# The joining products of the second image every fourth scan step and no longer every second

## The chip, the cores and the metric

The kernel runs on one core of a Trainium2 chip. The metric is the device time of one execution in microseconds, from launch to end; it includes little beside the span between the first and the last instruction. The engines are TensorE (PE), VectorE (DVE), ScalarE (ACT), GpSimd (POOL), and SyncE (SP), whose queue issues most of the DMA transfers. Each engine works through its own queue in program order, and waits at an instruction until what it depends on has been signalled.

## The reference, cut to what matters

The input x is (4, 256, 32, 32) in fp32: 4 images of 256 channels and 1024 tokens. One layer is a convolutional block with a residual, and then a layer of experts with a residual:

```python
x = x + conv_block(ln_over_channels(x))
t = tokens(x)                         # 4 x 1024 rows of 256
t = t + experts(layernorm(t))         # top 2 of 8, 256 -> 1024 -> 256, GELU

# conv_block, for each image
xn = layernorm(x)
xm = four mamba scans over 64 channels each (16 states) + skip * xn
... gates and convolutions along the tokens give xm2
x_local  = conv1d(xm2)                # over the tokens, per channel
x_global = attention(xm2)             # 8 heads, 1024 tokens
x_out = concat(x_local, x_global) @ fc_w.T + fc_b     # the joining product, 512 -> 256
x_out = gelu(layernorm(x_out))
xi = ln_over_the_image(x_out), then a 3x3 convolution per channel
x_mixed = layernorm(xi) @ proj_w.T + proj_b
```

## The kernel before, in words

**Layout.** Channels lie on the 128 partitions in two blocks (`c` or `co`), tokens along the free axis in two halves of 512 (`h`). One PSUM bank holds one 128x512 fp32 tile; the eight banks are handed out by `ps(name)` from one pool, each in turn as its last reader lets it go. Buffers of one half in SBUF come from `a2`, of 1024 tokens from `a4`, of both blocks from `a8`.

**The scan sets the tick.** The mamba scans of an image are 8 parts, four channel groups by two halves of the tokens, of 16 steps each (one state each). A step of a part is: ACT makes dA (L732), PE makes bs, the input factors (L724), DVE multiplies dBu (L742) and runs the recurrence (L753), POOL multiplies the result by the output factors (L761), and PE sums over the states (yp, L766 and L771). Round the parts come the smaller jobs of each channel group: up products and silu (L630 to L660, with its table load), softplus of dt on ACT (L675 to L678) and its sums on POOL (L682, L686).

**All else is laid between the steps.** The whole program is written in a manually ordered schedule: instructions are in each engine's queue in the order in which Python issues them. Every other job is a generator. After each scan step `beat()` raises the tick by one and lets each running generator go on until it yields; `yield n` means "not again for n steps". So a job's yields decide behind which scan step its instructions stand in each queue. Behind the fourth scan part of an image (from the second image on) the attention of the image before is started, then `joined`, in one chain. So the second image is joined in the third image's fifth part. Outside the scans (in the attention stage, and at the end) beats go on without steps.

**The joined product.** `joined(b)` makes four products (`CO_H`: two output blocks by two halves) with `in_turn`. Each product is four matmuls 128x128 by 128x512 (L428), into one PSUM bank; ACT copies it with a bias into `xc` (L1286). `in_turn` makes one item per turn, uses the one made `lag // every` turns ago, and yields `every` steps per turn. For the second image (b = 1) the lag is 4.

**What hangs on it.** After the last turn `joined` sets the flag `("joining", b)`. Then it takes the deviation over the channels (`inverse_deviation`: squares on ACT, mean on PE, `root` on ACT at L419 and L420, multiplies on DVE at L1269) and the Gelu (L1295, with a table load, and another back, L413). The flag also releases `sent_off(b - 1)`, that is `sent_off(0)` for image 1 when the second image is joined (`behind_flag`): it loads the residual xr (1 MB, L1361), takes off the mean and the deviation (L1355, L1269), makes the four proj products (`pr`, L426 and L428), whose copies add the bias on ACT (L1373). Then comes the dispatch to the experts: transposes of the rows (`raw`, L1836), their copies to XR on ACT (L1828), statistics on DVE (L1843, L1844), the store of Y, the gate product (L1867), the routing, and sixteen scatters of XR's rows to HBM on POOL's queue, one every two steps, each with a memset (L1974, L1975). POOL has these beside its scan multiplies of the end of the third image and the start of the fourth; there too lie the third image's convolutions, with taps on DVE (L462).

Of the kernel before, what the change touches and what calls it, by code (L numbers as in the profile page):

```python
# [78 lines left out]
def network(  # L79
# [46 lines left out]
    def col(name, i=0, rows=slice(0, P)):  # L126
        at = _AT[name] + i
        return V[rows, at : at + 1]
# [22 lines left out]
    with tc.tile_pool(name="w_conv", bufs=1) as wp, tc.tile_pool(  # L151
# [239 lines left out]
        def a8(name, shape=(P, NC2, N)):  # L391
            return act8.tile(list(shape), F32, tag="a8", name=name)
# [13 lines left out]
        def half(h):  # L406
            return ts(h, HALF)
# [3 lines left out]
        def log_exp():  # L411
            if loaded[0] != LOG_EXP:
                nc.scalar.preload_act_table_set(LOG_EXP)  # L413
                loaded[0] = LOG_EXP
# [7 lines left out]
        def product(name, w, co, chunks, kept=None, at=0):  # L422

            out = ps(name)
            if kept is not None:
                nc.tensor.matmul(out, ident, kept, start=True, stop=False)  # L426
            for ci, chunk in enumerate(chunks):
                nc.tensor.matmul(  # L428
                    out, w[:, at + ci, ts(co, P)], chunk, start=(ci == 0 and kept is None),
                    stop=(ci == len(chunks) - 1),  # L430
                )
            return out
# [10 lines left out]
        def in_turn(items, make, use, lag=2, every=1):  # L443

            made, lag = [], lag // every
            for at in range(len(items) + lag):
                if at >= lag:
                    use(items[at - lag], made[at - lag])
                if at < len(items):
                    made.append(make(items[at]))  # L450
                yield every
# [772 lines left out]
        def pace(b, ticks):  # L1224

            if b == B - 1:
                T["pace",] = ticks

        def inverse_deviation(name, xc, alone, quick=False):

            r = a4(f"r_{name}")

            def squares(h):
                sq = [a2(f"sq_{name}_{h}_{c}") for c in range(NC2)]
                for c in range(NC2):
                    nc.scalar.activation(sq[c], xc[:, c, half(h)], AF.Square)
                return sq

            if alone:
                sq = [squares(h) for h in range(2)]  # L1240
                var = []
                for h in range(2):
                    yield 1
                    var.append(column_mean(f"var_{name}_{h}", sq[h]))
                yield 1
                for h in range(2):
                    root(r[:, half(h)], var[h], eps5)
                yield 1
            elif quick:
                sq, var = [], []  # L1250
                for at in range(6):
                    if at < 2:
                        sq.append(squares(at))
                    if 2 <= at < 4:
                        var.append(column_mean(f"var_{name}_{at - 2}", sq[at - 2]))
                    if 4 <= at:
                        root(r[:, half(at - 4)], var[at - 4], eps5)
                    yield 1
            else:
                for h in range(2):  # L1260
                    sq = squares(h)
                    yield 1
                    var = column_mean(f"var_{name}_{h}", sq)
                    yield 2
                    root(r[:, half(h)], var, eps5)
                    yield 1
                yield 1
            for c in range(NC2):
                nc.vector.tensor_tensor(xc[:, c, :], xc[:, c, :], r, ALU.mult)  # L1269
                yield 1  # L1270

        def joined(b):

            xloc, oT = XLOC.pop(b), OT.pop(b)
            pace(b, PACE["product"])
            T["attending", b] = True
            while b == B - 2 and not T.get(("projected", b - 1)):
                yield 1
            xc = XC[b] = a8(f"xc_{b}")
            both = [xloc[:, ci, :] for ci in range(NC2)] + oT  # L1280
            yield from in_turn(
                CO_H, lambda at: product(
                    f"fc_{b}_{at[0]}_{at[1]}", fcT_s, at[0],
                    [v[:, half(at[1])] for v in both],
                ),
                lambda at, r: nc.scalar.activation(  # L1286
                    xc[:, at[0], half(at[1])], r, AF.Identity, bias=fcb[:, at[0] : at[0] + 1]
                ), lag=(4, 4, 2, 2)[b], every=(4, 2, 2, 1)[b],
            )

            T["joining", b] = True
            pace(b, PACE["norm"])
            yield from inverse_deviation(f"lgn_{b}", xc, b == B - 1)
            for c in range(NC2):
                nc.scalar.activation(  # L1295
                    xc[:, c, :], xc[:, c, :], AF.Gelu, bias=col("lgn_b", c), scale=col("lgn_w", c)
                )
            loaded[0] = None
            if b < B - 1:
                log_exp()  # L1300
            yield 2
# [280 lines left out]
        with tc.manual_schedule(engines=ALL):  # L1582
# [4 lines left out]
            for b in range(B):  # L1587
                for p in range(PARTS):
# [15 lines left out]
                    if b > 0 and p == PARTS // 2 - 1:  # L1604
                        drain()
                        start(
                            one_by_one(attention(b - 1), joined(b - 1)), finish_part(at),
                            one_by_one(
                                local(b - 1), *([around(b - 2)] if b > 1 else []),
                                *([normalised(b + 1)] if 1 < b < B - 1 else []),  # L1610
                            ),
                        )
                        if b == B - 1 and b in XD:
                            start(taps_ahead(b))
                        if b > 1:
                            flag = "attending" if b == B - 1 else "joining"
                            start(behind_flag((flag, b - 1), sent_off(b - 2)))
                        if b == 1:
                            start(normalised(b + 1))
                        while not T.get(("attended", b - 1)):  # L1620
                            beat()
                        resume(at + 1)
# [12 lines left out]
            until("attended", B - 1, 2)  # L1635
            T["hold",] = False
            start(one_by_one(joined(B - 1), around(B - 1), sent_off(B - 1)))
            if not shifted:
                start(judged())
# [912 lines left out]
```

## Time and profile before

| | us |
|---|---|
| median of 3 runs | 2160.07 |
| lowest, highest | 2158.35, 2161.26 |
| profiled execution, its own time | 2160.25 |
| its span, first to last instruction | 2158.5 |
| PE, DVE, ACT, POOL busy | 1921.5, 1539.0, 1212.5, 1052.9 |
| mean granted PE clock | 0.963 |

The profile is of one execution. A line of its timeline is: start, duration, engine, source line, operation, output and inputs, shape, count of instructions drawn together; in brackets, the idle time of the engine just before, and what ended it. In a line of windows, the columns are the stretch, its length, the busy time (and count) of PE, PE's weight loads, DVE, ACT and POOL, then the granted PE clock, the busy share of the DMA engines, and GB/s. The line with one digit per slice gives the busy share in tenths for 40 equal slices of the span. Instructions of one kind that follow each other are drawn as one line, and the ends of matmuls are modelled.

The four products stand at 906, 915, 920 and 927 us in the third image's fifth part; the transposes of the first image's dispatch begin at 987, its scatters lie between 1033 and 1108, and the fourth image's first scan step is at 1045.

### The profile page before, as it was taken

What the parts mean: (1) busy time and instruction counts of PE and PEld (TensorE: products, weight loads), DVE (VectorE), ACT (ScalarE), POOL (GpSimd) and SP (SyncE); (2) the same over time, 40 slices, a digit from 0 to 9 for tenths busy, and PEclk for the clock granted to TensorE, in tenths of its full rate; (3) what the DMA queues carried; (4) which work ended last, traced back from release to release, by engine and by line L of the source; (5) the groups of instructions that cost most, each with busy time, mean ns of one, the idle gap of its engine ahead of it and who ended that gap; (6) DMA issues with size and microseconds to landing.
All of it is one profiled execution on the core that took longest, in us unless ns stands there. A gap on an engine that the chain in (4) does not pass through costs nothing. (4 is left out here: it accounts for less than half of the span.)

```text
span 2158.5 us, 28179 instructions
## 1 busy us (share of the span) xinstructions
PE 1921.5 (89%) x8682; PEld 866.5 (40%) x8682; DVE 1539.0 (71%) x2253; ACT 1212.5 (56%) x2274; POOL 1052.9 (49%) x935
## 2 busy tenths in 40 slices
PE   6778778999887999988789999769999989999996
PEld 2112112322211232223123223226743768888885
DVE  3999999876999989789889898986265345221121
ACT  4665657678676667677466876625267423222221
POOL 0787887731887850376878016752031012422131
PEclk8888999999999999998999999999999999999998
DMA  3665544311454431053734203445230166877764
GB/s 99 152 161 127 125 122 102 90 41 50 105 117 122 94 85 40 17 133 98 187 87 108 80 6 98 109 162 146 81 92 23 47 198 172 233 230 189 212 185 131
DMA packets 157087, 251.40 MB, mean 116 GB/s; under 512 B 34740, under 2 KB 101332, under 8 KB 156664
## 3 DMA queue, kind: packets, MB, share of 16 engines
q1 hardware_dynamic: 136560, 223.47, 38.2%
q0 software_dynamic: 12720, 17.32, 4.1%
q10 hardware_dynamic: 7640, 8.65, 1.3%
q8 instruction: 72, 1.18, 0.2%
q14 instruction: 95, 0.78, 0.1%
HBM read 137.22 MB, written 36.62 MB: 81 GB/s over the span
## 5 line engine op out<-in xcount | busy, mean ns | idle before, releaser
L761 POOL TENSOR_TENSOR dA<-hs,cs 128x512 f32<-128x512 f32 x512 | 684.0, 1345 | 374.7 <-DVE hs L753 246.7
L732 ACT ACTIVATE dA<-dts,A 128x512 f32<-128x512 f32 x512 | 359.0, 718 | 152.6 <-DMA dts<-dt 68.8
L771 PE MATMUL yp<-dA,quads 128*32 128x512 f32 x1024 | 284.4, 631 | 87.5 <-POOL dA L761 72.8
L2382 POOL DMA_INDIRECT Y<-ys,dest x68 | 109.6, 1612 | 425.4 <-DVE ys L2375 418.4
L1150 ACT ACTIVATE e<-st 128x512 f32<-128x512 f32 x512 | 263.6, 605 | 86.8 <-PE st L1140 81.6
L2369 ACT ACTIVATE hs<-h,b 128x256 f32<-128x256 f32 (+1 forms) x256 | 110.2, 479 | 345.6 <-PE h L2364 241.3
L742 DVE TENSOR_TENSOR dBu<-dts,bs 128x512 f32<-128x512 f32 x384 | 259.8, 677 | 48.9 <-PE bs L724 14.5
L753 DVE TENSOR_TENSOR_SCAN hs<-dA,last,dBu 128x512 f32<-128x512 f32 x192 | 243.7, 1269 | 2.9 <-PE yp L771 1.1
L2397 PE MATMUL y<-w,hs 128*128 128x256 f32 (+1 forms) x1088 | 243.3, 382 | 0.7 <-issue 0.4
L2364 PE MATMUL h<-xT,w 128*128 128x256 f32 (+1 forms) x1024 | 239.6, 390 | 0.8 <-DVE xT L2327 0.8
L753 DVE TENSOR_TENSOR_SCAN hs<-dA,dBu 128x512 f32<-128x512 f32 x192 | 231.9, 1208 | 1.9 <-PE av L1162 1.3
L1200 DVE TENSOR_TENSOR e<-e,e 128x512 f32<-128x512 f32 x256 | 171.0, 729 | 74.7 <-ACT e L1150 45.7
L2397 PEld LDWEIGHTS y<-w,hs 128*128 128x128 f32 (+1 forms) x1088 | 197.2, 188 | 37.7 <-issue 9.8
L2364 PEld LDWEIGHTS h<-xT,w 128*128 128x128 f32 x1024 | 195.3, 192 | 41.9 <-issue 8.3
L2327 DVE COPY xT<-xp 128x512 f32<-128x512 f32 (+1 forms) x36 | 23.3, 647 | 246.2 <-PE xp L2323 245.9
L724 PE MATMUL bs<-u,xpwT_s 128*32 128x512 f32 x1024 | 157.4, 651 | 39.7 <-DVE hs L753 15.0
L1140 PE MATMUL st<-qk 32*128 32x512 f32 x1024 | 174.4, 638 | 1.3 <-DVE hs L753 1.2
L771 PEld LDWEIGHTS yp<-dA,quads 128*32 128x32 f32 x1024 | 50.6, 112 | 297.7 <-POOL dA L761 196.4
L1190 PE MATMUL av<-e,v 128*32 128x512 f32 x1024 | 138.6, 604 | 0.0
L1975 POOL DMA_INDIRECT XS<-XR,to x64 | 65.6, 1025 | 92.3 <-ACT e L1150 53.9
L1140 PEld LDWEIGHTS st<-qk 32*128 32x128 f32 x1024 | 60.1, 183 | 115.7 <-issue 87.1
L742 DVE TENSOR_TENSOR bs<-dts,bs 128x512 f32<-128x512 f32 x128 | 86.2, 673 | 0.9 <-DMA dts<-dt 0.9
(374 smaller groups left out, 2637.3 us busy)
## 6 DMA issues: line engine op xcount, KB each, us to landing
dts<-dt SPq DMA_DIRECT2D x512, 128.0 KB
w<-in_W_dram SPq DMA_DIRECT2D x124, 512.0 KB
cs<-cd SPq DMA_DIRECT2D x512, 64.0 KB
xs<-XS SPq DMA_DIRECT2D x32, 260.0 KB
xd<-xn SPq DMA_DIRECT2D x64, 128.0 KB
xn<-in_x_dram SPq DMA_DIRECT2D x8, 512.0 KB
XL<-xl SPq DMA_DIRECT2D x8, 512.0 KB
xl<-XL SPq DMA_DIRECT2D x4, 1024.0 KB
```

The source lines that it names most:

```text
L724: nc.tensor.matmul(bs[r], xpwT_s[:, n, s : s + 1].to_broadcast([P, 32]), T[b, n, "u"][:, half(h)], start=True, stop=True,)
L732: nc.scalar.activation(dA, T[b, n, h, "dts", g][:, 0, :], AF.Exp, scale=A[:, g, n, q : q + 1])
L742: nc.vector.tensor_tensor(dBu, T[b, n, h, "dts", g][:, 1, :], T[b, n, h, "bs", q], ALU.mult)
L753: nc.vector.tensor_tensor_scan(hs, T[b, n, h, "dA", i], dBu, 0.0 if h == 0 else last, ALU.mult, ALU.add)
L761: nc.gpsimd.tensor_tensor(dA, hs, T[b, n, h, "cs", q], ALU.mult)
L771: nc.tensor.matmul(T[b, n, h, "yp"][ts(g, 32)], quads, T[b, n, h, "dA", q * GD + g], start=False, stop=(q == GS - 1),)
L1140: nc.tensor.matmul(sts[i], k[r, ts(kt, P)], q[r, half(h)], start=True, stop=not shifted)
L1150: ins = nc.scalar.activation(es[i], sts[i], AF.Exp, scale=1.0 / HD**0.5)
L1190: nc.tensor.matmul(accs[0][ts(i, HD)], v8[:, kt, ts(4 * g + i, HD)], es[i], start=(kt == 0), stop=(kt == NK - 1),)
L1200: nc.vector.tensor_tensor(first[i], first[i], es[i], ALU.add)
L2364: nc.tensor.matmul(hp[:, i, :], w1(c, k0 + i), xT[:, c, :], start=(c == 0), stop=(c == NC2 - 1))
L2397: nc.tensor.matmul(yp[ts(k % parts, n), ts(t % 2, C)], hidden(k)[:, ds(t * P, n)], w2(k), start=(k < parts), stop=(k >= NHC - parts),)
```

## The change

One number is changed: for the second image `joined` now yields 4 steps per turn and no longer 2. The lag in the same line, 4 steps, stays; `lag // every` falls from 2 turns to 1.

```diff
                 lambda at, r: nc.scalar.activation(
                     xc[:, at[0], half(at[1])], r, AF.Identity, bias=fcb[:, at[0] : at[0] + 1]
-                ), lag=(4, 4, 2, 2)[b], every=(4, 2, 2, 1)[b],
+                ), lag=(4, 4, 2, 2)[b], every=(4, 4, 2, 1)[b],
             )
 
             T["joining", b] = True
```

The helper that reads these numbers, unchanged:

```python
def in_turn(items, make, use, lag=2, every=1):
    made, lag = [], lag // every
    for at in range(len(items) + lag):
        if at >= lag:
            use(items[at - lag], made[at - lag])
        if at < len(items):
            made.append(make(items[at]))
        yield every
```

## The prediction

> **What bounds the kernel now.** I read the busy shares of the whole span first, then the span by stretches, then VectorE's (DVE's) waits round the edited place, then the timelines of DVE, PE, ACT and POOL there.
>
> ```profile
> PE 1921.5 (89%) x8682; PEld 866.5 (40%) x8682; DVE 1539.0 (71%) x2253; ACT 1212.5 (56%) x2274; POOL 1052.9 (49%) x935
> ...
> DVE  3999999876999989789889898986265345221121
> ```
>
> PE has the largest share, but it is an average: each slice is 54 us, and from slice 2 to slice 27 DVE is at 8 or 9 tenths in most. The edit lies in slices 17 and 18. The windows of that stretch, with the columns time, PE, PEld, DVE, ACT and POOL:
>
> ```profile
> 910.00:1130.00 220.00, 179.24 (x675) 55.49 (x676) 197.43 (x256) 144.89 (x260) 174.02 (x152) 0.95 0.50 127
> 1032.00:1068.00 36.00, 26.40 (x97) 5.70 (x98) 35.60 (x42) 15.94 (x35) 34.28 (x40) 1.00 0.71 193
> ```
>
> DVE is busy 197.4 of 220 us. Its unit is the scan step, dBu (L742, 0.67) and scan (L753, 1.21 or 1.27): 1.71 us for a first half of the tokens, 1.77 for a second. The work is the same before and after, so the time can only change by what DVE waits for in these 22.6 us, or by instructions that run longer. Its four longest waits between 900 and 1130 us:
>
> ```profile
> 924.57 0.69 DVE L742 TENSOR_TENSOR dBu<-dts,bs 128x512 f32<-128x512 f32 x1 [5.36 <-PE bs L724]
> 983.38 0.70 DVE L742 TENSOR_TENSOR dBu<-dts,bs 128x512 f32<-128x512 f32 x1 [1.88 <-ACT xr L1373]
> 1080.09 0.69 DVE L742 TENSOR_TENSOR dBu<-dts,bs 128x512 f32<-128x512 f32 x1 [5.42 <-ACT g L958]
> 1093.22 5.45 DVE L462 SCALAR_TENSOR_TENSOR d<-xm,V,d 128x1024 f32<-128x1024 f32 x1 [4.02 <-ACT d L457]
> ```
>
> The first is the edited products' own: PE's timeline shows bs behind the third of them.
>
> ```profile
> 919.91 1.88 PE L428 MATMUL fc<-xloc,fcT_s 128*128 128x512 f32 x4
> 921.63 1.88 PE L428 MATMUL fc<-qk,fcT_s 128*128 128x512 f32 x4
> 923.44 1.06 PE L724 MATMUL bs<-u,xpwT_s 128*32 128x512 f32 x8
> ```
>
> **The sum's base.** The durations come from the profiled execution: span 2158.5, its own time 2160.25, against a median of 2160.07 (2158.35 to 2161.26). The difference is a fifth of a microsecond, so I add my sum to 2160.1. A change under 0.2%, 4.3 us, can't be told from none.
>
> **The change part by part.** No instruction is added or removed on any engine or queue; all are reordered, and the spacing of the steps themselves is untouched. in_turn divides the lag of 4 by the spacing: two turns of 2 steps become one turn of 4. A product still rests 4 steps before ACT copies it, but six turns of 2 become five turns of 4, so 12 steps become 20. Of the four products of 3.44 us the second, third and fourth come 2, 4 and 6 steps later, and the flag "joining" 8 steps later, with all that hangs on it: norm and Gelu of the second image, and sent_off(0) of the first with xr's load on SP's queue, mean, squares, proj products, then the dispatch with raw transposes, XR copies, the store of Y, gate, routing and the sixteen scatters on POOL's queue.
>
> 1. The products. The third product moves behind bs, so bs comes 3.44 us sooner (two groups of four matmuls, 1.72 each from start to start), and the 5.36 shrinks to 1.9. PE is busy without a break from 905 to 936; the moved products fill places that other moved work leaves, and I find no new wait. −3.4 (−4.5 to −2.5).
>
> 2. The wait of 1.88 for the residual and one of 0.21 for the first XR copy are at steps that the shift empties: −2.1 (−2.1 to 0, should the dBu there find another late bank).
>
> 3. The Gelu burst of the second image (load 1.28, two Gelus of 1.24, load 1.28) lands 8 steps later, behind a softplus. The PSUM bank that a dBu then wants is read by a root (L419, ACT) that is queued behind both loads and both Gelus. Counted by hand: +1.2 (0 to +3).
>
> 4. The chain of sent_off: DVE multiplies xi (L1269), PE makes the proj products, ACT copies with the bias (L1373), PE transposes (L1836), ACT copies XR (L1828), DVE takes its statistics (L1843). Before, this ran clear of ACT's next silu group; 8 steps later the XR copy is queued behind it, on ACT's timeline:
>
> ```profile
> 997.48 1.28 ACT L656 ACT_TABLE_LOAD   x1
> 998.77 1.27 ACT L656 ACTIVATE u<-up,V 128x512 f32<-128x512 f32 x2
> 999.93 1.06 ACT L660 ACTIVATE z<-z 128x1024 f32<-128x1024 f32 x1
> 1001.00 1.28 ACT L413 ACT_TABLE_LOAD   x1
> ```
>
> From the end of the second xi multiply PE's queue holds, by its rows of before: rest of a product 0.95, up pair 1.71, product 2.67, bs 0.88, yp 0.97, product 2.67, up pair 1.71, product 2.67: 14.2 us. Then ACT: a residual 0.7, the silu group 4.8 (the four rows), three dA of 0.7 and the XR copy of 0.6: 22.4 in all. DVE reaches its statistics after nine steps of 1.71, 15.4. So it waits +7.0 (+2 to +9; the low end if DVE comes there late itself, by the waits of items 3 and 5). Behind the waiting statistics stand all later scan steps.
>
> Here a rule of the Trainium skill speaks against the change more than the row. "ScalarE: Activation LUTs", section "What ACT_TABLE_LOAD costs", charges a switch about 1.28 for the load and about 1.38 for a drain. The row has the 1.28, and the next ACTIVATE starts 1.29 after the load began: no drain is seen. By the rule the two switches make the chain 2.8 longer, the wait 9.8 and the whole sum 2168. I take the row, and the rule's price as the high end.
>
> 5. PE's clock. Before that chain PE waits for the xi multiplies, by my count up to 3.3 us in one piece (before: 1.21 and 1.78). The nearest row is an idle of 2.77, on PE's timeline:
>
> ```profile
> 1089.13 2.07 PE L426 MATMUL fx<-xl,ident 128*128 128x512 f32 x2 [2.77 <-ACT over L676]
> 1091.00 2.53 PE L428 MATMUL fx<-d,fpwT_s 128*128 128x512 f32 x4
> ```
>
> The same pair takes 1.13 and 1.88 six us earlier, and the granted clock of 1089 to 1091 is 0.50. "TensorE: Matmul & The Clock Gate", section "What's actually happening", halves the clock after at least one idle window of about 3.4 us, by which 3.3 would cost nothing. Here it halved after 2.77, so the row decides: about 3.4 us of work at half clock, of which PE loses half: +2 (0 to +3).
>
> 6. POOL at the start of the fourth image's scans. From 1032 to 1068 POOL is busy 34.28 of 36 us, with scatters between its multiplies; one takes 1.32 of its queue, from the start of its memset to the next instruction (POOL's timeline):
>
> ```profile
> 1052.15 0.10 POOL L1974 MEMSET apart<- 128x1 f32 x1
> 1052.41 1.03 POOL L1975 DMA_INDIRECT XS<-XR,to  x1 [0.16 <-issue]
> 1053.47 1.27 POOL L779 TENSOR_TENSOR z<-y,z 128x512 f32<-128x512 f32 x1
> ```
>
> POOL's backlog ends, by way of yp, the gate and bs, in DVE's wait of 5.42 at 1080. Scatters follow each other every 2 steps, so 8 steps take four of them out of the front of this stretch; about one less stands in the backlog when the fourth image starts at 1045, and most of that is kept: −1.0 (−3 to 0).
>
> 7. The same four come out at the other end, 1109 to 1122, where POOL idles 0.80, 0.81, 0.44, 0.49, 0.56, 0.52 and 0.48, 4.1 us against 4 × 1.32 = 5.3 of scatters: 1.2 late. There DVE runs depthwise taps (L462) of 1.26; the same form took 5.45 at 1093 and 2.79 at 1100, where POOL ran without a gap. I take one slightly stretched tap: +1.5 (0 to +6).
>
> 8. SP's queue: xr's load of 1 MB is issued 8 steps later, behind one more cs load and just ahead of a dts load, and Y's store likewise. DMA is busy half of the time there, and DVE shows no DMA wait: 0 (0 to +3, the size of ACT's 3.17 wait for dts at 971).
>
> Sum: −3.4 − 2.1 + 1.2 + 7.0 + 2.0 − 1.0 + 1.5 = +5.2, so 2165.3.
>
> **The rivals.** *The chain is hidden* (0.23). If pr, residual, silu and XR copy together stay under DVE's 15.4, items 4 and 5 fall away: −3.8, 2156.3, or 2155 without item 3 as well. For it: DVE shows only 0.21 of waiting for XR now. Against it: 22.4 is far over 15.4, and the silu group alone is 4.8.
>
> *Late scatters strike the taps* (0.16), the worse of the slower sides. If POOL stays without a gap from 1109 to 1130, three taps (1109, 1121, 1125) run at 2.79 to 5.45 instead of 1.26: item 7 becomes 3 × 2.7 = +8, the whole 2172. It decides once the scatters need more than the 4.1 idle, which they do by 1.2; against it, the multiplies follow the scans there one by one and POOL soon catches up.
>
> *The gain is taken back at once* (0.06): the wait on bs was only one form of PE's debt, the moved products delay later bs by as much, and items 1, 2 and 4 cancel: 2160. PE is full up to 936, which speaks for it; the moved proj work that makes room speaks against it. That the change does not do what it says belongs here: the flag comes 8 steps later by the program's own order, so only the gain can be void.
>
> **How the numbers follow.** My own case has 0.55, with 2160 to 2171 from the ends of item 4 and half of the others'; a good quarter of it, 0.15, is under 2164.4. Faster: 0.14 of the hidden chain's 0.23, whose values lie round the bound of 2155.8, and 0.01 of the third rival, 0.15. Within 0.2%: 0.15 of my case, 0.09 of the hidden chain and 0.04 of the third rival, 0.28. Slower: 0.40 of mine, the scatters' 0.16 and 0.01, 0.57. The range 2156 to 2173 leaves out the far ends of the first two rivals, about 0.15.
>
> **What would show it.** At 924 DVE's wait for bs should be near 1.9; none for the residual at 983. A new wait of 5 to 8 us before a statistics instruction (L1843, for ACT's XR) between 995 and 1010 shows step 4, a granted clock under 0.7 in the proj products step 5, four scatters after 1109 step 7. I am wrong if DVE waits under 2 us there, if a new wait for bs over 3 us follows within 925 to 940, or if the taps after 1109 take over 2.5 each.

## The result, and the profile after

| | before | after |
|---|---|---|
| median of 22 runs, us | 2161.53 | 2165.03 |
| lowest, highest | 2157.24, 2165.96 | 2160.65, 2166.94 |
| span of the profiled execution | 2158.5 | 2164.8 |
| mean granted PE clock | 0.963 | 0.956 |

The ratio is 1.0013, with a 95% interval of 1.0007 to 1.0018: 1.5 to 3.9 us slower, 2.8 in the middle. That is less than the 0.2%, or 4.3 us, below which the prediction calls a change none, though the interval does not reach 1: a small loss, of which the size is known only roughly. The two medians lie 3.5 us apart; the two profiled spans differ by 6.3, but 1.3 of this was there before the first edited instruction (the scan step at 914.44 us in the profile of before is at 915.72 in that of after). Single executions of one kernel differ by several us, mostly in stages that this edit does not touch. I therefore read the traces from that scan step on.

The page's engine row and DVE's slices of after say only that nothing large moved:

```profile
PE 1923.5 (89%) x8682; PEld 867.7 (40%) x8682; DVE 1541.9 (71%) x2253; ACT 1212.6 (56%) x2274; POOL 1051.7 (49%) x935
...
DVE  3999998976998989798989889986265355321211
```

The windows of the same two stretches, with the columns as before, show POOL with 25 of 36 us where it had 34 (the scatters begin later), and PE at a mean granted clock of 0.91 and 0.76 where it had 0.95 and 1.00:

```profile
910.00:1130.00 220.00, 177.37 (x659) 55.76 (x658) 195.89 (x250) 140.74 (x254) 170.82 (x150) 0.91 0.48 123
1032.00:1068.00 36.00, 25.70 (x83) 5.95 (x82) 35.44 (x59) 19.66 (x42) 25.08 (x27) 0.76 0.57 146
```

DVE's timeline of after has the new waits, in the brackets, two multiplies that take longer, and last the old wait for the gates (g), which stays:

```profile
919.04 0.70 DVE L742 TENSOR_TENSOR dBu<-dts,bs 128x512 f32<-128x512 f32 x1 [2.11 <-ACT xc L1286]
...
924.29 2.25 DVE L572 TENSOR_TENSOR xn<-xn,r 128x1024 f32<-128x1024 f32 x1
...
979.13 0.70 DVE L742 TENSOR_TENSOR dBu<-dts,bs 128x512 f32<-128x512 f32 x1 [1.08 <-ACT r_fin L419]
...
980.87 2.10 DVE L1269 TENSOR_TENSOR xi<-xi,r_fin 128x1024 f32<-128x1024 f32 x1
...
993.79 0.70 DVE L742 TENSOR_TENSOR dBu<-dts,bs 128x512 f32<-128x512 f32 x1 [0.98 <-PE bs L724]
...
998.11 0.70 DVE L742 TENSOR_TENSOR dBu<-dts,bs 128x512 f32<-128x512 f32 x1 [2.50 <-ACT xr L1373]
...
1004.98 0.70 DVE L742 TENSOR_TENSOR dBu<-dts,bs 128x512 f32<-128x512 f32 x1 [1.49 <-ACT u L656]
...
1009.23 0.43 DVE L1843 BATCH_NORM_STATS2 st<-XR 128x6 f32<-128x256 f32 x1 [2.42 <-ACT XR L1828]
...
1085.70 0.70 DVE L742 TENSOR_TENSOR dBu<-dts,bs 128x512 f32<-128x512 f32 x1 [5.42 <-ACT g L958]
```

In before, the same multiply of xn and the wait for the first XR copy were:

```profile
926.31 1.20 DVE L572 TENSOR_TENSOR xn<-xn,r 128x1024 f32<-128x1024 f32 x1
...
988.83 0.43 DVE L1843 BATCH_NORM_STATS2 st<-XR 128x6 f32<-128x256 f32 x1 [0.21 <-ACT XR L1828]
```

The 5.36 for bs is gone, and so are the 1.88 and the 0.21 at their places: 7.45 us. In their place stand 2.11, 1.08, 0.98, 2.50, 1.49 and 2.42: 10.58. That is +3.1 of waiting. Another +2.0 is longer instructions: one multiply of xi (L1269) takes 2.10 and not 1.19, one of xn (L572) 2.25 and not 1.20, each begun while a POOL multiply runs, as it was not in before. About 0.2 is spread over many. At the fourth image's first scan step after is 5.3 us later than before, counted from the step at 914; after that comes −1.0 at POOL's backlog and +0.9 at the taps.

The four waits from 993 to 1009 are one chain. First PE, then ACT, on their timelines of after:

```profile
985.87 2.07 PE L428 MATMUL pr<-xi,projT_s 128*128 128x512 f32 x2 [1.72 <-DVE xi L1269]
987.73 1.56 PE L630 MATMUL up<-xd,inwk 128*128 128x512 f32 x2
...
998.05 1.02 PE L636 MATMUL up<-xd,inwk 128*128 128x512 f32 x2
998.91 1.02 PE L426 MATMUL pr<-xr,ident 128*128 128x512 f32 x2
999.76 1.88 PE L428 MATMUL pr<-xi,projT_s 128*128 128x512 f32 x4
```

```profile
1001.68 0.69 ACT L1373 ACTIVATE xr<-pr,prb 128x512 f32<-128x512 f32 x1 [2.92 <-PE pr L428]
1002.39 1.28 ACT L656 ACT_TABLE_LOAD   x1
...
1005.91 1.28 ACT L413 ACT_TABLE_LOAD   x1
...
1008.62 0.58 ACT L1828 COPY XR<-raw 128x512 f32<-128x512 f32 x1
```

The silu group's last input, the up product of 998.05, is done at 999.1, but the group is queued behind the last residual, which waits until 1001.68 for the last proj product. The XR copy is queued behind the group. From the end of the second xi multiply (985.8) to the end of the XR copy are 23.4 us; 22.4 were predicted.

### The profile page after: what moved, and what is told of

It is laid out like the page before. It is cut to its first block, busy times and chain, and to the rows that moved or that the text cites. A ratio compares the mean times of both kernels' runs of the same rounds, so it can differ in the third digit from the quotient of the medians.

```text
span 2164.8 us, 28177 instructions
## 1 busy us (share of the span) xinstructions
PE 1923.5 (89%) x8682; PEld 867.7 (40%) x8682; DVE 1541.9 (71%) x2253; ACT 1212.6 (56%) x2274; POOL 1051.7 (49%) x935
```

## The experiments

Each kernel was timed against the kernel before on the same chip. In the table, "timed" is the difference from the ratio with its 95% interval, times 2161 us; "trace" is the shift of DVE's scan step of before's 1113.17 against its scan step of 914.44, in one profiled execution. The first trace of the change has +4.3.

| kernel | timed, us | trace, us |
|---|---|---|
| a0, the change | +2.4 (+0.9 to +4.1) | +2.9 |
| e1, flag early | −5.2 (−7.1 to −3.0) | −4.4 |
| e2, sent_off late | +3.0 (+1.3 to +4.5) | +5.7 |
| e3, norm and Gelu late | −3.0 (−4.5 to −1.3) | −2.3 |
| e4, sent_off 4 late | +2.6 (+0.6 to +4.5) | +3.1 |
| e5, sent_off 12 late | −6.9 (−9.9 to −3.9) | −6.2 |
| e6, dispatch 8 late | −6.7 (−8.4 to −5.2) | −5.7 |
| e7, scatters 8 late | −4.3 (−6.5 to −2.2) | −5.4 |
| e8, e4 with the idle filled | −2.4 (−4.3 to −0.4) | −1.0 |
| e9, no silu tables | +1.1 (−1.1 to +3.2) | +1.4 |
| e10, every 3 | −4.3 (−6.3 to −2.4) | −0.9 |
| e11, dispatch 12 late | −7.8 (−10.8 to −4.8) | −9.0 |

The trace column stops short of two things that the times include. The first is the taps on DVE: one of them takes 2.9 us and not 1.26 in both traces of the change and in e2, e7, e9 and e10, and two of them in e5 and e11. Counted on to before's scan step of 1144.82, the shifts of e5 and e11 are only −3.6 and −6.4, that of e1 is −5.2 and that of e6 −4.4. The second is a wait for bs a few steps later: about 2.8 us in e1, e3, e4, e5, e6, e7, e9 and e11, 1.2 in the first trace of the change and in e8, at most 0.2 in the others. Ahead of it the granted clock is 0.50 in e1 (1125 to 1130) and 1.00 in before (1134 to 1139). Whether the edits or chance made that clock stays open.

**a0, the change again.**

> The changed kernel again, beside the three that follow, on the same chip. All theories: +1.5 to +4 us against the kernel before (ratio 1.0007 to 1.0018), as in the result. In its trace the wait of 5.36 for bs behind the third joining product should be gone again, with about 2.1 for a bank of the joining product's copy in its place.

Ratio 1.0011 (1.0004 to 1.0019). The trace repeats the first one (2.11, 1.07, 1.93, 1.50, 2.42) but for two things: no wait of 0.98 for bs, and 1.93 for the residual and not 2.50, together 1.6 less. PE's timeline of a0 at that place:

```profile
985.63 1.13 PE L428 MATMUL pr<-xi,projT_s 128*128 128x512 f32 x2 [1.72 <-DVE xi L1269]
986.59 1.02 PE L630 MATMUL up<-xd,inwk 128*128 128x512 f32 x2
```

The groups took 2.07 and 1.56 in the first profile of after. The windows of 985 to 990, first of a0, then of that profile:

```profile
985.00:990.00 5.00, 4.37 (x10) 2.01 (x11) 4.97 (x7) 1.89 (x5) 3.83 (x3) 1.00 0.55 120
```

```profile
985.00:990.00 5.00, 4.13 (x7) 1.87 (x8) 4.97 (x7) 2.22 (x5) 3.83 (x3) 0.66 0.61 134
```

After the same idle of 1.72 the clock is 1.00 in one execution and 0.66 in the other. So a lowered clock is part of this kernel's loss in some executions only.

**e1 to e3, the change in its three parts.** The change delays the products, the second image's own norm and Gelu, and sent_off(0). e1 leaves sent_off(0) where it was, counted in steps:

```diff
+            def made_at(at):
+                if b == 1 and at == CO_H[-1]:
+                    T["joining", b] = True          # 12 steps after the first
+                return product(...)
-                CO_H, lambda at: product(...)
+                CO_H, made_at,
```

> The joining products come every 4 steps, but the flag that releases sent_off(0) is set where it was, 12 steps after the first product; only the second image's own norm and Gelu are 8 steps later. Theory A (the products gain about 3.3 us at their place, the loss is sent_off's chain run into the silu group): 2 to 3.5 us faster than before, a ratio near 0.999. Rival B (the gain at the products is given back at once, or the late Gelu makes the loss): no faster than before, 0 to +3 us.

Ratio 0.9976 (0.9967 to 0.9986): faster by more than theory A had it. In its trace the waits of 5.36, 1.88 and 0.21 are gone and only the 2.12 for the joining product's bank is new. The changed kernel differs from e1 in the start of sent_off(0) alone, and is 7.6 us slower by the ratios. The loss of the change is thus not in the products.

```diff
             if b == B - 2:
                 yield 6
+            if b == 0:
+                yield 8                             # e2, in sent_off
```

> The joining products stay every 2 steps and the second image's norm and Gelu stay where they were; sent_off(0) alone starts 8 steps later. Theory A: the 5.36 for bs stays, and the chain's loss comes without the gain: +5 to +7 us (ratio 1.0025 to 1.003). Rival B (all of the change's +2.8 is sent_off's, the products give nothing): +2.8 us. Rival C (the loss is the Gelu's): 0.

Ratio 1.0014 (1.0006 to 1.0021), which is rival B's +2.8; theory A's +5 to +7 lies outside the interval. The trace has theory A's waits (5.36 stays; 1.23, 2.51, 1.49 and 2.43 come) and a shift of 5.7, outside what was timed. Its execution had a granted clock of 0.78 and 0.88 in the two stretches of 5 us with the proj products; whether that explains the whole difference stays open. Timed, e2 and the change can't be told apart (+3.0 and +2.4), so that the times show no gain at the products. The traces do: 5.36 goes and 2.12 comes, in e1 and in the change.

```diff
             T["joining", b] = True
+            if b == 1:
+                yield 8                             # e3, in joined
```

> The joining products and the flag stay; only the second image's own norm and Gelu come 8 steps later. Theory A: one new wait of about 1 us behind the Gelu's table loads, +0 to +1.5 us. Rival C (the Gelu burst behind the softplus makes the loss): +2.5 us or more.

Ratio 0.9986 (0.9979 to 0.9994), a miss of both: it is faster by 3 us. DVE's timeline shows why. In before, the two multiplies of the second image's xc stand ahead of the two of xi:

```profile
957.37 1.19 DVE L1269 TENSOR_TENSOR xc<-xc,r_lgn 128x1024 f32<-128x1024 f32 x1
...
960.27 1.19 DVE L1269 TENSOR_TENSOR xc<-xc,r_lgn 128x1024 f32<-128x1024 f32 x1
...
966.71 1.19 DVE L1269 TENSOR_TENSOR xi<-xi,r_fin 128x1024 f32<-128x1024 f32 x1
...
969.62 1.19 DVE L1269 TENSOR_TENSOR xi<-xi,r_fin 128x1024 f32<-128x1024 f32 x1
```

In e3 they stand behind:

```profile
960.02 1.19 DVE L1269 TENSOR_TENSOR xi<-xi,r_fin 128x1024 f32<-128x1024 f32 x1
...
962.93 1.19 DVE L1269 TENSOR_TENSOR xi<-xi,r_fin 128x1024 f32<-128x1024 f32 x1
...
969.38 1.20 DVE L1269 TENSOR_TENSOR xc<-xc,r_lgn 128x1024 f32<-128x1024 f32 x1
...
972.22 1.20 DVE L1269 TENSOR_TENSOR xc<-xc,r_lgn 128x1024 f32<-128x1024 f32 x1
```

So 2.4 us of DVE's own work moved from ahead of the chain xi, proj, residual into the time in which the chain runs, and the waits of 1.88 and 0.21 at the chain's end are gone. In the change both moved together, the order of the four multiplies is the old one, and nothing of this is gained. By the traces e1 is e3's gain and the products' gain together: −2.2 as in e3's, and −2.2 at the products (5.36 less, 2.12 and one longer multiply more). By the times alone e1 and e3 do not differ for certain; their intervals overlap.

**e4 to e7, how late and what.** All four stand on e1.

```diff
+            if b == 0:
+                yield 4                             # e4; 12 in e5; in sent_off
...
+            if b == 0:
+                yield 8                             # e6: behind the proj products
...
+        if b == 0:
+            yield 8                                 # e7: ahead of the scatters
```

> As e1 (joining products every 4 steps, flag as before the change), but sent_off(0) starts 4 steps later and not 0 or 8. The root of its norm is still queued ahead of the Gelus on ACT, and three of its four XR copies ahead of the silu group. Theory A (the loss is the chain norm, proj, XR copies meeting ACT's two table-switching groups): most of e1's gain stays, 2 to 5 us faster than before. Rival D (the later sent_off starts, the more it costs, whatever it meets): half way from e1 to the change, 0 to -2 us.

> As e1, but sent_off(0) starts 12 steps later. Its root is queued behind the Gelus, its residual copies meet the silu group and the XR copies come clear behind it. Theory A: the waits that the change has in the XR copies fall away, but the residual copies are late behind the silu group: 0 to +3 us against before, not more than the change. Rival D: worse than the change, +4 to +7 us.

> As e1, but only from behind the proj products on (transposes, XR copies, routing, scatters) is sent_off(0) 8 steps later; its norm and proj products stay on time. Theory A: PE has made the last product long before the silu group, so the transposes can stand ready and DVE's statistics wait at most for the silu group: of the four waits (1.0, 2.5, 1.5, 2.4) that the change shows only the last can remain, 0 to 2.5 us slower than e1, so 3 to 5 us faster than before. Rival E (the dispatch's late routing and scatters are the loss): as slow as the change, +2 to +4.

> As e1, but only the sixteen scatters on POOL start 8 steps later. Theory A: a gain of about 0.9 at the fourth image's first parts and a loss of about 0.9 at the taps after 1109, together within 1 us of e1. Rival E (late scatters strike the taps): 3 us or more slower than e1, taps of over 2.5 each in the trace.

e4: ratio 1.0012 (1.0003 to 1.0021), and e5: 0.9968 (0.9954 to 0.9982). The expectations of both theories fell for both: 4 steps cost as much as 8, and e5 with 12 is no slower than e1, within the noise. e7 (0.998, 0.997 to 0.999) came as theory A had it, and e6 (0.9969, 0.9961 to 0.9976) went past it, 6.7 us faster where 3 to 5 were told; both speak against rival E. In e6 transposes and XR copies stand at the same steps as in the change, behind the same silu group with the same two table loads, and DVE shows no wait for any of them. Here is its first XR copy on ACT, behind the second load, and then its first statistics on DVE, without a wait (in the edited kernels the line numbers are a few higher):

```profile
996.27 1.28 ACT L413 ACT_TABLE_LOAD   x1
...
998.98 0.57 ACT L1836 COPY XR<-raw 128x512 f32<-128x512 f32 x1
```

```profile
1000.97 0.40 DVE L1851 BATCH_NORM_STATS2 st<-XR 128x6 f32<-128x256 f32 x1
```

So the XR copies behind the silu group are harmless by themselves; in the change they are late because the proj products are. e5's proj products begin right behind the last up product, and DVE waits 0.82, 1.93 and 0.31 in all that stretch. PE's timeline of e5:

```profile
987.85 1.02 PE L636 MATMUL up<-xd,inwk 128*128 128x512 f32 x2
988.71 1.02 PE L426 MATMUL pr<-xr,ident 128*128 128x512 f32 x2
```

In e4 and in the change, up products and the proj products share the same steps of PE's queue. That meeting is what e4 and the change have, and e5 and e6 have not. It is not the whole of e4's loss, as e8 shows, and e5 owes a part of its time to POOL: its six late scatters leave the waits of 5.42 and 1.6 at 3.98 and none, and make two taps longer.

In e4 two waits for bs stand out, of 3.22 and 3.10 us. The first one is the clock's. PE's timeline of e4:

```profile
978.03 2.08 PE L428 MATMUL pr<-xi,projT_s 128*128 128x512 f32 x2 [2.85 <-DVE xi L1269]
980.04 2.07 PE L643 MATMUL zp<-xn,inzT_s 64*128 64x512 f32 x2
982.04 2.08 PE L426 MATMUL pr<-xr,ident 128*128 128x512 f32 x2
983.91 3.16 PE L428 MATMUL pr<-xi,projT_s 128*128 128x512 f32 x4
987.00 1.06 PE L724 MATMUL bs<-u,xpwT_s 128*32 128x512 f32 x8
```

Every group up to bs takes about twice its time, and the window of 978 to 983 has a granted clock of 0.50:

```profile
978.00:983.00 5.00, 4.96 (x5) 1.50 (x6) 4.96 (x6) 4.89 (x10) 5.00 (x5) 0.50 0.04 13
```

**e8, the idle time filled.** The first proj product's residual matmuls are made three times and its first chunk twice, into the same bank and in the time in which PE would idle; the last ones count:

```diff
+            if name == "pr_0_0_0":
+                nc.tensor.matmul(out, ident, kept, start=True, stop=True)
+                nc.tensor.matmul(out, ident, kept, start=True, stop=False)
+                nc.tensor.matmul(out, w[:, at, ts(co, P)], chunks[0], start=False, stop=True)
             if kept is not None:
                 nc.tensor.matmul(out, ident, kept, start=True, stop=False)
```

> As e4 (sent_off 4 steps later), where PE idles 1.13 and 2.85 us for the two xi multiplies ahead of the first proj product, and then runs at a granted clock of 0.50 for 5 us; DVE then waits 3.22 for bs. Here the first product's residual matmuls are made three times over and its first chunk twice, with the same result: 2.6 us more of PE work, laid in those idle times. Theory G (the half clock makes that wait): the clock stays over 0.9, the 3.22 is gone, 2 to 3.5 us faster than e4, so 0 to -2 against before. Rival H (the wait is PE's amount of work there): no faster than e4 or slower, +2.5 to +4 against before.

Ratio 0.9989 (0.998 to 0.9998): e4's +2.6 became −2.4, by doing more work. On PE's timeline of e8 the same groups now run at full speed:

```profile
976.12 1.12 PE L434 MATMUL pr<-xi,projT_s 128*128 128x512 f32 x2 [1.14 <-DVE xi L1275]
977.17 1.12 PE L649 MATMUL zp<-xn,inzT_s 64*128 64x512 f32 x2
978.23 1.12 PE L432 MATMUL pr<-xr,ident 128*128 128x512 f32 x2
979.19 1.88 PE L434 MATMUL pr<-xi,projT_s 128*128 128x512 f32 x4
981.00 1.06 PE L730 MATMUL bs<-u,xpwT_s 128*32 128x512 f32 x8
```

and the window of 975 to 980 has a clock of 1.00:

```profile
975.00:980.00 5.00, 3.88 (x8) 1.46 (x9) 4.97 (x6) 4.98 (x9) 5.00 (x4) 1.00 0.01 3
```

From the first of these groups to bs are 4.9 us where e4 had 9.0, and the wait of 3.22 is gone. The second stays, at 2.35: in e8 PE works from 981 to 995 without a break, at a granted clock of 1.00, and up products stand between the last proj product and that bs. So this wait is the amount of work that meets there. Rival H is out for the first wait and right for the second; of e4's loss the clock is the larger part.

**e9, the silu group without tables.** In the fourth image's first channel group silu is an identity, and the two table loads fall away:

```diff
-                    u[:, half(h)], T[b, n, h, "up"], AF.Silu, bias=col("convb", n)
+                    u[:, half(h)], T[b, n, h, "up"],
+                    AF.Identity if (b, n) == (3, 0) else AF.Silu, bias=col("convb", n)
```

> The changed kernel, but in the fourth image's first channel group silu is left out (an identity, which needs no other table), so that ACT's two table loads of 1.28 fall away just where the change's residual and XR copies meet them. Theory A (chain of late proj products, residual, silu group, XR copy): the last two of the change's four waits, 1.5 for u and 2.4 for XR, shrink by 2.5 together or more; 2.5 to 4 us faster than the change, so about -1 to +0.5 against before. Rival I (PE alone is late, ACT's group is hidden): as slow as the change, +2 to +3.

Ratio 1.0005 (0.9995 to 1.0015). The interval reaches into both expectations, so the times don't settle it; the trace does. The wait for u (1.49) is gone, and that for XR is down to

```profile
1006.72 0.43 DVE L1848 BATCH_NORM_STATS2 st<-XR 128x6 f32<-128x256 f32 x1 [1.00 <-ACT XR L1833]
```

while the 0.92 for bs and the 2.50 for the residual stay as they were. Against the first trace of the change, 2.9 us of the waits were thus ACT's group behind the late residual (1.49, and 1.42 of the 2.42), and 3.5 were PE's late proj products (0.98 and 2.50).

**e10 and e11, better versions.** e10 is e6 with `every=(4, 3, 2, 1)[b]`, the flag again 12 steps after the first product. e11 is e6 with 12 for 8.

> A version from what was found: as e6 (flag early, dispatch 8 steps later behind the proj products), but the joining products come every 3 steps. Their banks are copied a step sooner. If the new wait of 2.1 for a joining product's bank shrinks with that, 7 to 8.5 us faster than before; if PE's products then stand before bs again, 4 to 6 us faster and no better than e6.

> As e6, but the dispatch behind the proj products is 12 steps later and not 8, so that six scatters fewer lie on POOL ahead of the fourth image's gates (in e5, with as many, the wait of 5.42 for g had come down to 3.98 and the one of 1.6 for bs was gone). If POOL's backlog is what e5 gained by, 1 to 3 us faster than e6, 8 to 9.5 us faster than before; if e5's gain lay elsewhere, the same as e6.

e10: 0.998 (0.9971 to 0.9989), no better than e6. The 2.12 did not shrink (a root of the fourth image's own input norm, L419, took the place of the copy), and 1.19 for bs and 3.05 for a residual are new. e11: 0.9964 (0.995 to 0.9978), the best that was run, 7.8 us faster than before and 10.6 than the changed kernel by the ratios. Its interval overlaps with e6's, so the times do not show that it beats e6. Its trace has what was expected of POOL: the wait of 1.6 for bs is gone, and the one at the gates is shorter, but two taps now take 2.92 and 2.84:

```profile
1071.28 0.70 DVE L742 TENSOR_TENSOR dBu<-dts,bs 128x512 f32<-128x512 f32 x1 [3.98 <-ACT g L958]
```

## Why the prediction was right or wrong

The forecast was slower, 2165.3 us, and 2165.03 was measured. But a part of this is luck: the forecast was +5.2 on 2160.1, and the measured step is +2.8 (+1.5 to +3.9) on 2161.5. Up to the last tap of that stretch, the first trace of the change has +5.2 and the second +3.8. By the prediction's own bound of 4.3 us a step of 2.8 is none, a case to which it gave 0.28; slower had 0.57. So the direction and most of the mechanism were right, and the size too large by about two. By its own items:

1. The products, −3.4: the third one moved behind bs as told, and bs came 3.3 us sooner, counted from the step at 914. The 1.9 that was to be left does not stand at bs but two steps ahead of it, as 2.11 for a bank of the joining product, whose copy stands behind a root on ACT; 5.36 for 2.11 is −3.3. So "I find no new wait" failed, but cost next to nothing. What it missed is the multiply of xn that met a POOL at work (+1.05). Measured with it −2.1 in two traces of the change. PE's timeline of after has bs ahead of the third product:

```profile
921.43 1.06 PE L724 MATMUL bs<-u,xpwT_s 128*32 128x512 f32 x8
...
925.10 1.88 PE L428 MATMUL fc<-xloc,fcT_s 128*128 128x512 f32 x4
```

2. The waits of 1.88 and 0.21, −2.1: they went from their steps. I had taken them to be tied to these. e3 shows that they are tied to the order of the four multiplies: there they vanish although sent_off(0) starts where it did. In the change the order is the old one, and waits for the same two tiles, the residual and XR, stand in item 4, larger. So items 2 and 4 are one account: the chain was moved, and not its waits removed.
3. The Gelu burst, +1.2: measured 1.08 and 1.07, for r_fin, as told.
4. The chain, +7.0, as one wait at the statistics: it came as 0.98, 2.50, 1.49 and 2.42, together 7.4, and 5.9 in a0. The chain's length was right by 1.0 in 22.4. That it would bite first at bs and at the residual's bank, and that PE's part is the larger, I did not see: I put the whole wait behind the silu group, which by e6 is harmless alone, and the sign I named, one wait of 5 to 8 us at the statistics, did not come. As to the table load's price: in after, the ACTIVATE behind the load of 1002.39 starts 1.29 later, as in before. The drain that the Trainium skill charges ("ScalarE: Activation LUTs", section "What ACT_TABLE_LOAD costs") is not to be seen here either.
5. The clock, +2, on top of item 4: this term was mis-sized, at up to 1.4 in one trace and nothing in the other; and without it item 4 is 5.9 (a0) and not 7.0. PE's longest idle time ahead of the chain was 1.72 us in one piece, and not 3.3. A lower clock, 0.66, came in one execution of two; the two traces differ by 1.4 us. That PE can lose its clock after well under 3.4 us of idle in one piece, which the Trainium skill ("TensorE: Matmul & The Clock Gate", section "What's actually happening") would not have, e4 and e8 show: 2.85 and 1.13 us of idle, then 0.50, and 1.00 when they are filled.
6. POOL's backlog, −1.0: −1.0 in both traces, but the 5.42 stayed to the hundredth; what went were small waits ahead of it. With four scatters fewer ahead of it, it did not move; in e5 and e11, with six fewer, it fell to 3.98.
7. The taps, +1.5: one tap of 2.91 and not 1.26, less a wait of 0.63 that went with it, +0.9.
8. SP's queue, 0: DVE shows no wait for a transfer there.

The sum of the traces is then −2.1 for item 1, −2.1, +1.1, +5.9 to +7.4 with the clock in it, +0.9 for the longer multiply of xi, −1.0 and +0.9, or +3.6 to +5.1. Why the timed +2.4 to +2.8 lies at the low end of this, one profiled execution each can't say.

Of the rivals, the hidden chain is out (four waits), the scatters at the taps are out for this change (one tap of 2.91, and e7), though 12 steps make two such taps in e5 and e11, and the gain at the products was not taken back at once, as the traces of e1 and of the change show.

## What to carry to other kernels

A chain that runs over several engines costs by what it meets more than by how late it is: 0, 4, 8 and 12 steps of delay gave −5.2, +2.6, +2.4 and −6.9 us. Of the 7.8 us between 0 and 4 steps 5.0 was the clock, as e8 shows. Move a flag's dependents separately from the work that sets the flag, and put the bound engine's own work behind the start of a chain and not ahead of it, so that it fills the time in which the chain runs. When a wait on PE seems to be too much work, look at the granted clock first: more work in the idle time made e4 5 us faster by the ratios.

## What the hardware showed that I had not expected

- After idle times of 1.13 and 2.85 us on PE, with 1.12 of work between them, the granted clock was 0.50 for 5 us (e4). After 1.72 us of idle, with 2.25 of 5 us busy before it, it was 0.66 in one execution of the changed kernel and 1.00 in another.
- Where one of DVE's multiplies of xn, xc or xi overlapped with a POOL multiply, the one that started later was stretched, at all twelve such places of before and after. In after, POOL's from 980.63 took 1.26, DVE's from 980.87 2.10, and POOL's next one, from 981.85, 2.25; in before, DVE's from 966.71 took 1.19 and POOL's from 966.94 2.10. A shift of a quarter of a microsecond decided which engine paid.
- An XR copy queued behind an ACT group with two table loads of 1.28 us cost DVE nothing (e6).
